# Routing, last rows and send requests of a fused two-layer kernel moved to the ends of attention steps

## The chip, the cores and the metric

The kernel runs on one core of one Trainium2 chip. The metric is the device time of one execution in microseconds; for the kernel before, the median of three runs. Five engines work side by side: TensorE (PE; its weight loads are PEld), VectorE (DVE), ScalarE (ACT), GpSimd (POOL) and SyncE (SP), which issues most of the DMAs.

## What is computed

The reference is two layers on 4096 tokens (8 batches of 512) of width 256. Each layer normalizes its rows and adds an attention-like block and a mixture of experts to them:

```python
xn = _layernorm(x, axis=-1)
x = x + _L0_attn_ref(xn, ...) + _L0_ffn_ref(xn, ...)
xn = _layernorm(x, axis=-1)
x = x + _L1_attn_ref(xn, ...) + _L1_ffn_ref(xn, ...)
return x
```

The first layer's block is a two-directional state-space scan, its experts take one of eight per token. The change concerns the second layer. Its attention has 16 heads of width 16, with keys and values that pass through a latent of width 64:

```python
latent_kv = (k + v) @ W_down_kv
k_rec = latent_kv @ W_up_k
v_rec = latent_kv @ W_up_v
scores = clip(einsum('bhqd,bhkd->bhqk', qh, kh) * scale) * decay
attn = softmax(clip(scores), axis=-1)
out = einsum('bhqk,bhkd->bhqd', attn, vh)
return out @ Wo
```

Its mixture of experts takes the two best of eight per token; the eighth is a "no operation" that returns the token itself, weighted. Each of the seven real experts takes at most 512 tokens, in order of their index:

```python
weights_flat = softmax(x @ router_w.T + router_b, axis=-1)
topk_vals, topk_idx = top_k(weights_flat, 2)
sorted_indices = argsort(-expert_mask, axis=0)[:cap]
h = relu(einsum('ceh,ehi->cei', inputs, experts_inter))
out = einsum('cei,eih->ceh', h, experts_out) * in_w[..., None]
combined = zeros_like(x_flat).at[used_idx].add(out)
combined = combined + x_flat * (noop_w * noop_mask)[:, None]
```

## The kernel before, in words

All data are 32-bit floats. A tile holds 128 tokens (32 tiles, four per batch). The order of instructions on every engine is the order in which Python emits them: generators are advanced by hand, one piece (from one `yield` to the next) at a time, and each engine works its own instructions off in that order, waiting where an operand is not ready.

**The end of the first layer.** `late()` (L512 to 594) finishes the rows of each batch: it adds the gathered expert output (L549), takes mean and variance (L551, L552), writes the rows `x1` (L560), normalizes (square root L159 on ScalarE, L164 to L169 and L567 on VectorE), writes the normalized rows `xn1` (L570), transposes them (L575, L576), and projects to the router's logits (`pp` L582, `proj1` L587). The pieces for batch 7 are left when the second layer begins; they are the generator `rest`.

**The attention steps.** The second layer's loop (L1411 to L1468) goes over 128 steps n = (batch b, head group g of four heads, query tile c), and three more to drain. A step issues, in order: the scores of step n (`scores`, L1277: four matmuls `s_ps` L1284 into four PSUM banks, on VectorE four clips L1289, four products with the decay `band` with a running maximum L1291, and one negation `ng` L1295); one piece of each running `divide` chain; `follow()`; then the exponentials of step n-1 on ScalarE (`exps`, L1299), the transposes of step n-2 (`p_ps` L1306 on TensorE, copies `pT` L1307 on ScalarE), on every second step the products with V (`o_ps` L1315); and between these three or four calls of `fill()`. A clip frees a PSUM bank for the next step's scores.

**What fills.** `fill()` (L1372) advances the first of three lists: a group that may not be split, `urgent`, `idle`. In `urgent` stand first the batch-7 rows (`last_rows`, L1367, put in at L1407), later `inputs_of(b + 1)` from step n = 8 of each 16 (the next batch's latent `lp` L235, Q, K and V; the Q and K rows are stored and read back by `spread`, L1173, one store and 16 small DMAs on SP each), and `finish(b)` (L1224, output projection `fin` L1228, sum L1232). `idle` gets the experts. All these use one PSUM tile with the tag "bank", `bufs=1`: a new use waits until the last reader of the previous one is done.

**Routing and sending.** `follow()` (L1389) does nothing until the batch-7 rows are done. Then each call advances `route1()` (L1074) by one piece: bias and softmax (`softmax_experts`, L174; the exponential L180 on ScalarE), the first maximum (`first_max`, L186), the second, the mask, the ranks (`ranks`, L198: two matmuls `both` L203 and L204 into "bank", a copy of the totals L206, a running sum over tiles L211 and L212, and a last read of `both` in L217), and twice the slots and weights (L1112 to L1116). When routing is done, each call advances `send_rows()` (L1190) twice. Its first piece asks on SP for all eight batches of both `x1` (L1200) and `xn1` (L1197), 512 KB each; each further piece takes a tile: a copy of its slots (`at`, L1221), two indirect DMAs on POOL into `xd1` (L1208), and on VectorE the no-operation share (L1215), which needs both loads. After the last tile `ready` is set and the first expert's weights and rows are asked for (L1129, L1124).

**The divide chain.** After a head group's last product with V, `divide` (L1321) copies the sums out (`os` L1325), stores them (`od` L1326), two steps of the chain later reads them back (`oT` L1336, `sm` L1337), takes the reciprocal (L1342), stores it (`rd` L1343), reads it back spread over the rows (`rb` L1345), and two steps on multiplies (L1348). Its DMAs stand on SP.

**Experts and the end.** From step `ready + 2` the experts are in `idle`: transposes `e_tp` L1144, `e_hp` L1151, `e_yp` L1164. When nothing is left to fill, `more()` (L1385) advances `combine()` (L1242): two gathers on POOL per tile (L1249); the additions (`add`, L1260, at L1263) lag seven tiles behind, and the last seven tiles' 14 additions come in one go.

Of the kernel before, what the change touches and what calls it, by code (L numbers as in the profile page):

```python
# [49 lines left out]
def bc(ap, axis, shape):  # L50

    return ap.unsqueeze(axis).to_broadcast(shape)
# [3 lines left out]
def tile_kernel(ctx: ExitStack, tc: tile.TileContext, t, out: bass.AP):  # L56
# [54 lines left out]
    def rows_of(src, b):  # L111
        return src[b * S : (b + 1) * S, :].rearrange("(c p) d -> p c d", p=P)
# [61 lines left out]
    def softmax_experts(pool, logits, bias):  # L174
        pr = pool.tile(E3, FP, name="pr", tag="pr")
        V.tensor_tensor(pr, logits, bc(bias, 1, E3), ALU.add)
        m = pool.tile([P, NTILE], FP, name="sm_m", tag="sm_m")
        V.tensor_reduce(m, pr, AX.X, ALU.max)
        V.tensor_tensor(pr, pr, bc(m, 2, E3), ALU.subtract)
        A.activation(pr, pr, AF.Exp)  # L180
        V.tensor_reduce(m, pr, AX.X, ALU.add)
        V.reciprocal(m, m)
        V.tensor_tensor(pr, pr, bc(m, 2, E3), ALU.mult)
        return pr

    def first_max(pool, pr, tag):  # L186

# [7 lines left out]
        V.tensor_tensor(oh, bc(i, 2, E3), bc(iota_e, 1, E3), ALU.is_equal)  # L195
        return m, oh

    def ranks(pool, bank, mask):  # L198

        flat = mask.rearrange("p t e -> p (t e)")  # L200
        both = bank("both", [P, 2, NTILE * NE], 1)
        pre, tot = both[:, 0, :], both[:, 1, :]
        T.matmul(pre, row_lt, flat, start=True, stop=True)  # L203
        T.matmul(tot, ones, flat, start=True, stop=True)  # L204
        total = pool.tile(E3, FP, name="rk_t", tag="rk_t")
        V.tensor_copy(total, tot.rearrange("p (t e) -> p t e", e=NE))  # L206
        cum = total
        sh = 1
        while sh < NTILE:
            nxt = pool.tile(E3, FP, name="rk_c", tag="rk_c", bufs=2)  # L210
            V.tensor_copy(nxt[:, 0:sh, :], cum[:, 0:sh, :])  # L211
            V.tensor_tensor(nxt[:, sh:, :], cum[:, sh:, :], cum[:, : NTILE - sh, :], ALU.add)  # L212
            cum = nxt
            sh *= 2
        rank = pool.tile(E3, FP, name="rk_r", tag="rk_r")
        V.tensor_tensor(rank, cum, total, ALU.subtract)
        V.tensor_tensor(rank, rank, pre.rearrange("p (t e) -> p t e", e=NE), ALU.add)  # L217
        n = pool.tile([P, NE], FP, name="rk_n", tag="rk_n")
        V.tensor_copy(n, cum[:, NTILE - 1, :])
        return rank, n  # L220
# [98 lines left out]
    def bank(name, shape, tag="gen"):  # L319
        return mp.tile(shape, FP, name=name, tag=("e", "s")[tag] if isinstance(tag, int) else tag, bufs=2)  # L320
# [4 lines left out]
    def route():  # L325
# [49 lines left out]
        V.tensor_tensor(da, dt, bc(ea, 1, D3), ALU.mult)  # L375


        pr = softmax_experts(big, proj[:, :, 2 * NH :], br)
        m, oh = first_max(big, pr, "a")
        V.tensor_copy(gate, m)  # L380
        rank, n = ranks(big, bank, oh)
        over = big.tile([P, NE, NTILE], FP, name="over", tag="over")
        V.tensor_tensor(over, bc(n, 2, [P, NE, NTILE]), bc(iota_t, 1, [P, NE, NTILE]), ALU.is_gt)
        nb = big.tile([P, NE], FP, name="nb", tag="nb")
# [61 lines left out]
    with ExitStack() as es:  # L446
# [509 lines left out]
        with tc.manual_schedule(engines=ENGINES):  # L956
# [34 lines left out]
            def fill(n):  # L991
                for _ in range(n):
                    if next(rows, "end") == "end":
                        next(rest, None)
# [69 lines left out]
    with tc.tile_pool(name="a1", bufs=1) as p1, tc.tile_pool(name="a2", bufs=2) as p2, tc.tile_pool(  # L1064
# [9 lines left out]
        def route1():  # L1074

            nonlocal r1b, noop
            tls.close()
            big = r1b = r1s.enter_context(tc.tile_pool(name="r1b", bufs=1, side="right"))
            noop = r1b.tile([P, NTILE], FP, name="noop", tag="noop")
            pr = softmax_experts(big, proj1, rb)  # L1080
            yield
            m1, oh1 = first_max(big, pr, "a")

            rest = big.tile(E3, FP, name="rest", tag="rest")
            V.tensor_scalar(rest, oh1, -2.0, None, ALU.mult)
            V.tensor_tensor(rest, rest, pr, ALU.add)
            yield
            m2, oh2 = first_max(big, rest, "b")
            yield
            mask = big.tile(E3, FP, name="mask", tag="mask")  # L1090
            for m, oh in ((m1, oh1), (m2, oh2)):
                pos = big.tile([P, NTILE], FP, name="pos", tag="pos")
                V.tensor_scalar(pos, m, 0.0, None, ALU.is_gt)
                V.tensor_tensor(oh, oh, bc(pos, 2, E3), ALU.mult)
            V.tensor_tensor(mask, oh1, oh2, ALU.add)
            yield
            rank, _ = ranks(big, lambda name, shape, tag: bank(name, shape), mask)
            yield


            V.tensor_tensor(noop, pr[:, :, NE1], mask[:, :, NE1], ALU.mult)


            valid = big.tile(E3, FP, name="valid", tag="valid")
            V.tensor_scalar(valid, rank, float(CAP), None, ALU.is_lt)
            G.memset(valid[:, :, NE1 : NE1 + 1], 0.0)
            base = big.tile([P, NE], FP, name="base", tag="base")
            V.tensor_scalar(base, iota_e, float(CAP), float(NE * CAP - NSLOT1), ALU.mult, ALU.add)
            V.tensor_tensor(rank, rank, bc(base, 1, E3), ALU.add)
            for k, (m, oh) in enumerate(((m1, oh1), (m2, oh2))):  # L1110
                yield
                V.tensor_tensor(oh, oh, valid, ALU.mult)  # L1112
                sl = slots_of(big, oh, rank, "k")
                V.tensor_scalar(sl, sl, float(NSLOT1), None, ALU.add)
                V.tensor_copy(slot1[:, :, k], sl)
                V.tensor_copy(wsel[k], slots_of(big, oh, pr, "w"))  # L1116
# [73 lines left out]
        def send_rows():  # L1190

            sent = []
            rows = {}

            def ask(b):
                rows[b] = r1b.tile([P, TPB, DM], FP, name="xs", tag="xs", bufs=B)
                Y.dma_start(out=rows[b], in_=rows_of(xn1, b))  # L1197

            for b in range(B):
                Y.dma_start(out=x_sb[:, b * TPB : (b + 1) * TPB, :], in_=rows_of(x1, b))  # L1200
                ask(b)
            yield
            for i in range(NTILE):
                b, c = i // TPB, i % TPB
                x = rows[b][:, c, :]
                at = turn(r1b, i)
                for k in range(2):
                    one = G.indirect_dma_start(  # L1208
                        out=xd1, out_offset=bass.IndirectOffsetOnAxis(ap=at[:, k : k + 1], axis=0),
                        in_=x, in_offset=None, bounds_check=NSLOT1 - 1, oob_is_err=False,  # L1210
                    )
                    for other in sent:
                        tc.declare_no_dep(one.ins, other.ins, reason="rows go to slots of their own")
                    sent.append(one)
                V.scalar_tensor_tensor(x_sb[:, i, :], x, noop[:, i : i + 1], x_sb[:, i, :], ALU.mult, ALU.add)  # L1215
                yield
# [139 lines left out]
        with tc.manual_schedule(engines=ENGINES):  # L1356
# [4 lines left out]
            urgent, idle, chains = [], [], []  # L1361
            rows, routing, sends, work, ready, e1 = combine(), route1(), send_rows(), None, None, None

            half_done = []
            late_left = True

            def last_rows():  # L1367
                nonlocal late_left
                yield from rest
                late_left = False  # L1370

            def fill():  # L1372

# [9 lines left out]
                return False  # L1383

            def more():  # L1385
                if ready is not None and n > ready + 2:
                    next(rows, None)

            def follow():  # L1389

                nonlocal work, ready, e1, e2
                if late_left:
                    return
                if next(routing, "end") != "end":
                    return
                for _ in range(2):
                    if next(sends, "end") == "end" and ready is None:
                        ready = n
                        r1s.close()
                        e1 = es.enter_context(tc.tile_pool(name="f1", bufs=1, side="right"))  # L1400
                        e2 = es.enter_context(tc.tile_pool(name="f2", bufs=2, side="right"))
                        work = experts()
                        next(work)

            steps = [(b, g, c) for b in range(B) for g in range(4) for c in range(TPB)]
            N = len(steps)
            urgent.append(last_rows())  # L1407
            done = []
            pT, op, pair = {}, {}, None
            inputs = {0: got}  # L1410
            for n in range(N + 3):  # L1411
# [17 lines left out]
                for chain in list(chains):  # L1429
                    if next(chain, "end") == "end":  # L1430
                        chains.remove(chain)
                follow()
                if ready is not None and n == ready + 2:
                    idle.append(work)
                begun = n >= 1
                if begun:
# [29 lines left out]
                    fill() or more()  # L1466
                if 1 <= n <= N:
                    done[n - 1].exps((3,))  # L1468
            while fill() or chains:
                for chain in list(chains):  # L1470
                    if next(chain, "end") == "end":
                        chains.remove(chain)
# [76 lines left out]
```

## Time and profile before

| | us |
|---|---|
| three runs | 2246.86, 2250.88, 2252.46 (median 2250.88) |
| the profiled execution | 2233.12 |
| its span | 2231.4 |
| PE busy | 1935.2 (87%) |
| DVE busy | 1499.0 (67%) |
| ACT busy | 1070.2 (48%) |
| POOL busy | 689.8 (31%) |
| attention steps begin | 1172.2 |
| `ng` of step 0, 28, 111, 127 | 1182.39, 1432.18, 2088.73, 2198.03 |

The profile is of one execution. Its page gives the busy time of each engine, the span in 40 slices with each engine's busy tenths and the granted TensorE clock, the chain of waits that ended last, and the costliest groups of instructions. Other views give the same for a stretch of time, and the timeline lists instructions with the idle time before them and what ended it. The second layer's attention takes 1172 to 2231 us. `ng` (L1295) is issued once per step and so marks the steps.

### The profile page before, as it was taken

The page shows a single profiled execution, that of the slowest core. Times are in us where ns is not written, and L with a number is a line of the kernel's source. Part 1 is how long each engine was busy: PE and PEld are TensorE (multiplying, and loading weights), DVE is VectorE, ACT ScalarE, POOL GpSimd, SP SyncE. Part 2 cuts the span into 40 slices and gives each one's busy share as a digit, 9 for nine tenths or more (in the row PEclk, how much of TensorE's full clock was granted, in tenths as well). Part 3 has the DMA queues.
Part 4 walks back from the last instruction along what each step waited for, and adds up shares of the span by engine and source line. Part 5 has one row for each costly group of instructions (what it writes and reads, how often), then busy time and mean ns, then how long its engine had stood idle before and what let it go on. Part 6 is the DMA issues. An engine that isn't in the chain of part 4 may idle for free. (4 is left out here: it accounts for less than half of the span.)

```text
span 2231.4 us, 32949 instructions
## 1 busy us (share of the span) xinstructions
PE 1935.2 (87%) x11772; PEld 1281.0 (57%) x11772; DVE 1499.0 (67%) x3323; ACT 1070.2 (48%) x1978; POOL 689.8 (31%) x588
## 2 busy tenths in 40 slices
PE   6559999999998999987867768899999999999885
PEld 5325666667766676644544334565656656565543
DVE  4835766657585665678646679565666767676895
ACT  2223332323233242333324546676667777777764
POOL 0075554546364463655420035200000000000452
PEclk9879999999999999997885878799999999999978
DMA  7134544545454464343432161312213222222255
GB/s 263 38 103 160 174 157 162 193 141 203 139 172 150 132 212 143 128 128 114 157 100 67 37 212 61 96 53 84 71 46 101 82 67 78 58 86 58 90 110 97
DMA packets 156357, 263.61 MB, mean 118 GB/s; under 512 B 25146, under 2 KB 112622, under 8 KB 144290
## 3 DMA queue, kind: packets, MB, share of 16 engines
q1 hardware_dynamic: 124544, 144.65, 20.9%
q0 software_dynamic: 22320, 107.55, 14.9%
q10 hardware_dynamic: 9330, 9.31, 1.2%
q8 instruction: 93, 1.52, 0.3%
q14 instruction: 70, 0.57, 0.1%
HBM read 193.39 MB, written 72.75 MB: 119 GB/s over the span
## 5 line engine op out<-in xcount | busy, mean ns | idle before, releaser
L1289 DVE TENSOR_SCALAR s<-s_ps 128x512 f32<-128x512 f32 x512 | 317.4, 681 | 255.9 <-PE s_ps L1284 209.0
L1299 ACT ACTIVATE s<-s,ng 128x512 f32<-128x512 f32 x512 | 355.3, 727 | 51.7 <-DVE ng L1295 50.1
L1306 PE MATMUL p_ps<-ident,s 128*128 128x128 f32 x2048 | 296.0, 289 | 60.5 <-ACT pT L1307 60.5
L1306 PEld LDWEIGHTS p_ps<-ident,s 128*128 128x128 f32 x2048 | 244.7, 147 | 143.7 <-ACT pT L1307 94.3
L1291 DVE CUSTOM_DVE_ANT_0 s<-s,band 128x512 f32<-128x512 f32 x512 | 322.3, 683 | 0.0
L1307 ACT COPY pT<-p_ps 128x512 f32<-128x512 f32 x512 | 277.8, 591 | 56.3 <-PE p_ps L1306 52.1
L1249 POOL DMA_INDIRECT yg<-yd,at x64 | 67.6, 1056 | 700.6 <-PE s_ps L1284 654.3
L667 PE MATMUL pj<-xT,w_in 128*128 128x512 f32 x384 | 194.6, 632 | 19.4 <-DVE cv L680 18.3
L1284 PE MATMUL s_ps<-kT,qT 16*128 16x512 f32 x1024 | 181.5, 706 | 22.6 <-DVE s L1289 16.5
L486 PEld LDWEIGHTS h_ps<-xdT,w 128*128 128x128 f32 x1248 | 151.6, 195 | 32.6 <-issue 18.0
L486 PE MATMUL h_ps<-xdT,w 128*128 128x128 f32 x1248 | 156.7, 280 | 9.4 <-ACT xdT L476 8.3
L499 PE MATMUL y_ps<-w,hT 128*128 128x256 f32 x624 | 149.3, 382 | 0.7 <-DVE hT L495 0.7
L680 DVE SCALAR_TENSOR_TENSOR cv<-pj,w_conv_w,cv 128x511 f32<-128x511 f32 (+2 forms) x192 | 143.1, 745 | 7.4 <-ACT cv L676 3.4
L1315 PE MATMUL o_ps<-pT,vt 128*32 128x256 f32 x2048 | 143.2, 424 | 0.0
L898 POOL TENSOR_TENSOR yT<-yT,ex 128x512 f32<-128x512 f32 (+1 forms) x48 | 59.4, 1237 | 254.1 <-DVE ex L897 191.6
L499 PEld LDWEIGHTS y_ps<-w,hT 128*128 128x128 f32 x624 | 116.9, 192 | 35.7 <-issue 20.3
L887 DVE TENSOR_TENSOR yT<-yT,yd 128x512 f32<-128x512 f32 (+1 forms) x64 | 43.7, 682 | 122.6 <-PE yd L878 122.5
L667 PEld LDWEIGHTS pj<-xT,w_in 128*128 128x128 f32 x384 | 71.6, 200 | 92.1 <-issue 81.9
L1151 PE MATMUL e_hp<-e_xdT,e_w 128*128 128x256 f32 x448 | 122.4, 396 | 2.3 <-ACT e_xdT L1145 1.9
L835 POOL TENSOR_TENSOR au<-da,row_le 128x1024 f32<-128x1024 f32 x32 | 62.5, 1954 | 195.0 <-DVE end L387 94.1
L1164 PE MATMUL e_yp<-e_w,e_hT 128*128 128x256 f32 x448 | 120.0, 390 | 0.2
L855 ACT ACTIVATE mt<-seg 128x1024 f32<-128x1024 f32 x64 | 65.6, 1024 | 106.7 <-PE seg L850 106.6
(261 smaller groups left out, 3219.0 us busy)
## 6 DMA issues: line engine op xcount, KB each, us to landing
ex<-exd SPq DMA_DIRECT2D x96, 128.0 KB
u<-in_u_dram SPq DMA_DIRECT2D x16, 512.0 KB
xtd<-xT SPq DMA_DIRECT2D x16, 512.0 KB
fr<-fdd SPq DMA_DIRECT2D x64, 128.0 KB
od<-os SPq DMA_DIRECT2D x32, 256.0 KB
xT<-xtd SPq DMA_DIRECT2D x15, 512.0 KB
e_w<-in_ei_dram SPq DMA_DIRECT2D x7, 1024.0 KB
e_w<-in_eo_dram SPq DMA_DIRECT2D x7, 1024.0 KB
```

The lines of the kernel that those rows point to most:

```text
L486: T.matmul(hp[:, i, :], w1[:, k * FF + f * P : k * FF + (f + 1) * P], xdT[:, k * P : (k + 1) * P], start=(k == 0), stop=(k == KC - 1),)
L499: T.matmul(yp, hT[f // 4][:, f % 4, :], w2[:, f * DM : (f + 1) * DM], start=(f == 0), stop=(f == FC - 1))
L667: T.matmul(pj, w_in[:, k, o * P : (o + 1) * P], self.xT[:, k, :], start=(k == 0), stop=(k == KC - 1))
L680: V.scalar_tensor_tensor(cv[:, s:], pj[:, : S - s], conv_w[:, q, 3 - s : 4 - s], cv[:, s:], ALU.mult, ALU.add)
L1151: T.matmul(hp, w1[:, k, f * P : (f + 1) * P], xdT[:, k, :], start=(k == 0), stop=(k == KC - 1))
L1284: T.matmul(sp[i], self.q[r, cols], self.k[r, :], start=True, stop=True)
L1289: V.tensor_scalar(self.p[i], sp[i], -CLAMP, CLAMP, ALU.max, ALU.min)
L1291: V.tensor_tensor_reduce(out=self.p[i], in0=self.p[i], in1=band[:, at : at + S], scale=1.0, scalar=-3.0e38, op0=ALU.mult, op1=ALU.max, acc ...
L1299: A.activation(self.p[i], self.p[i], AF.Exp, bias=self.ng[:, i : i + 1])
L1306: T.transpose(pp[:, k, :], self.p[i][:, k * P : (k + 1) * P], ident)
L1307: A.copy(pT[i][:, :, cc * P : (cc + 1) * P], pp)
L1315: T.matmul(op[32 * i : 32 * i + 32, half * 2 * P : (half + 1) * 2 * P], self.v[:, k, h * (AD + 1) : h * (AD + 1) + 32], pT[i][:, k, :], st ...
```

## The change

Four things are moved or altered; the arithmetic stays the same.

1. `follow()` is called at the end of a step, after the last exponential, instead of before the fills. While batch-7 rows are left, it advances them itself, two pieces per step (`LATE`), so that they no longer stand in `urgent`; their first piece (the request for rows) is emitted before step 0.
2. `softmax_experts` yields ahead of its exponential. `route1` is cut anew, into six pieces instead of eight: the first maximum goes with the rest of the softmax; the second maximum with the mask; the ranks with the first part of the slots.
3. `ranks` copies all of `both` to SBUF at once (`hold` gives the place) and works from the copy.
4. `send_rows` asks for two batches at first, and for batch b + 2 when it comes to batch b's first tile. `xn1` is asked for ahead of `x1`.

The experts start at `ready + 3`, and `more` from `ready + 4`, since `ready` is now set at the end of a step.

```diff
@@ softmax_experts
         V.tensor_tensor(pr, pr, bc(m, 2, E3), ALU.subtract)
+        yield
         A.activation(pr, pr, AF.Exp)
...
-        return pr
+        yield pr
@@ ranks
-    def ranks(pool, bank, mask):
+    def ranks(pool, bank, mask, hold):
...
-        pre, tot = both[:, 0, :], both[:, 1, :]
-        T.matmul(pre, row_lt, flat, start=True, stop=True)
-        T.matmul(tot, ones, flat, start=True, stop=True)
-        total = pool.tile(E3, FP, name="rk_t", tag="rk_t")
-        V.tensor_copy(total, tot.rearrange("p (t e) -> p t e", e=NE))
+        T.matmul(both[:, 0, :], row_lt, flat, start=True, stop=True)
+        T.matmul(both[:, 1, :], ones, flat, start=True, stop=True)
+        held = hold([P, 2, NTILE * NE])
+        V.tensor_copy(held, both)
+        pre, total = (held[:, k, :].rearrange("p (t e) -> p t e", e=NE) for k in range(2))
@@ route1
-            pr = softmax_experts(big, proj1, rb)
+            chances = softmax_experts(big, proj1, rb)
+            next(chances)
             yield
+            pr = next(chances)
             m1, oh1 = first_max(big, pr, "a")
+            yield
...
             V.tensor_tensor(rest, rest, pr, ALU.add)
-            yield
             m2, oh2 = first_max(big, rest, "b")
-            yield
...
-            rank, _ = ranks(big, lambda name, shape, tag: bank(name, shape), mask)
-            yield
+            rank, _ = ranks(
+                big, lambda name, shape, tag: bank(name, shape), mask,
+                lambda shape: big.tile(shape, FP, name="rk_b", tag="rk_b"),
+            )
@@ send_rows
             def ask(b):
                 rows[b] = r1b.tile([P, TPB, DM], FP, name="xs", tag="xs", bufs=B)
                 Y.dma_start(out=rows[b], in_=rows_of(xn1, b))
-
-            for b in range(B):
                 Y.dma_start(out=x_sb[:, b * TPB : (b + 1) * TPB, :], in_=rows_of(x1, b))
+
+            for b in range(2):
                 ask(b)
             yield
             for i in range(NTILE):
                 b, c = i // TPB, i % TPB
+                if c == 0 and b + 2 < B:
+                    ask(b + 2)
@@ the loop of attention steps
+            LATE = (2, 2, 2, 2, 2)
...
-            def last_rows():
+            def last_rows(k):
+
                 nonlocal late_left
-                yield from rest
-                late_left = False
+                for _ in range(k):
+                    if next(rest, "end") == "end":
+                        late_left = False
...
             def more():
-                if ready is not None and n > ready + 2:
+                if ready is not None and n > ready + 3:
                     next(rows, None)
...
                 if late_left:
+                    last_rows(LATE[n])
                     return
...
-            urgent.append(last_rows())
+            last_rows(1)
...
-                follow()
-                if ready is not None and n == ready + 2:
+                if ready is not None and n == ready + 3:
                     idle.append(work)
...
                 if 1 <= n <= N:
                     done[n - 1].exps((3,))
+                follow()
```

The first layer's use of `softmax_experts` and `ranks` is adapted to the new signatures; there the whole copy goes into one of the existing row buffers.

More of the change, by code (lines that the diff above doesn't have):

```diff
@@ L216, in ranks @@
         V.tensor_tensor(rank, cum, total, ALU.subtract)
-        V.tensor_tensor(rank, rank, pre.rearrange("p (t e) -> p t e", e=NE), ALU.add)
+        V.tensor_tensor(rank, rank, pre, ALU.add)
         n = pool.tile([P, NE], FP, name="rk_n", tag="rk_n")
@@ L375, in route @@
         V.tensor_tensor(da, dt, bc(ea, 1, D3), ALU.mult)
-        pr = softmax_experts(big, proj[:, :, 2 * NH :], br)
+        _, pr = softmax_experts(big, proj[:, :, 2 * NH :], br)
         m, oh = first_max(big, pr, "a")
         V.tensor_copy(gate, m)
-        rank, n = ranks(big, bank, oh)
+        rank, n = ranks(big, bank, oh, lambda shape: row("rk_b").rearrange("p (a b) -> p a b", a=2))
         over = big.tile([P, NE, NTILE], FP, name="over", tag="over")
```

## The prediction

> **What bounds the kernel now.** I read the page's slices first, then the stages' table, then the chain of waits over 1140 to 1440 us, and last the timeline around each long piece of it.
>
> ```profile
> span 2231.4 us, 32949 instructions
> ...
> PE   6559999999998999987867768899999999999885
> ...
> PEclk9879999999999999997885878799999999999978
> ```
>
> Slices 22 to 26, some 1172 to 1437 us, are the weak spot: TensorE is 6 to 8 tenths busy at a granted clock of 5 to 8 tenths. That is the start of the second layer, attention steps 0 to 28, before its experts have begun: the stage that the change rearranges. The stages' table says what bounds what follows (after the range: length, then busy us of PE, PEld, DVE, ACT, POOL, then clock, DMA share, GB/s):
>
> ```profile
> 1244.00:1333.00 89.00, 58.49 (x357) 31.49 (x360) 55.94 (x164) 41.42 (x76) 14.59 (x15) 0.77 0.47 148
> ...
> 1437.00:2089.00 652.00, 626.12 (x4476) 409.62 (x4480) 435.50 (x1115) 470.35 (x905) 4.26 (x4) 0.98 0.22 71
> 2089.00:2232.00 143.00, 103.84 (x745) 59.87 (x736) 116.20 (x315) 84.69 (x153) 63.30 (x60) 0.84 0.53 107
> ```
>
> From 1244 to 1333 nobody is full: waits. From 1437 to 2089, with experts, TensorE is full (626 of 652), so moving work there saves nothing. After 2089 VectorE leads. The chain of waits names the waits of the first stage:
>
> ```profile
> 1248.34 6.75 issue
> 1255.09 3.54 PE lp L235 x4
> ...
> 1291.53 6.81 DMA xs<-xn
> ...
> 1313.32 8.43 DMA rd<-sm
> 1321.77 4.38 DMA rb<-rd
> ```
>
> The timeline shows who stands there (brackets: idle time just before, and what ended it):
>
> ```profile
> 1218.34 0.42 ACT L180 ACTIVATE pr<-pr 128x256 f32<-128x256 f32 x1 [7.45 <-issue]
> ...
> 1254.57 0.42 DVE L217 TENSOR_TENSOR rk_r<-rk_r,both 128x256 f32<-128x256 f32 x1
> 1255.09 3.54 PE L235 MATMUL lp<-xT,w_kv 128*64 128x512 f32 x4 [6.76 <-issue]
> ...
> 1298.44 0.48 DVE L1215 SCALAR_TENSOR_TENSOR x_sb<-xs,noop,x_sb 128x256 f32<-128x256 f32 x1 [6.02 <-DMA xs<-xn]
> ...
> 1326.27 0.69 DVE L1348 TENSOR_TENSOR oT<-oT,rb 128x512 f32<-128x512 f32 x1 [10.13 <-DMA rb<-rd]
> ...
> 1437.08 1.09 PE L1144 MATMUL e_tp<-ident,e_xd 128*128 128x128 f32 x4 [5.67 <-DMA rd<-sm]
> ...
> 2198.11 5.06 DVE L1263 SCALAR_TENSOR_TENSOR x_sb<-yg,wsel,x_sb 128x256 f32<-128x256 f32 x11
> ```
>
> ScalarE stands 7.45 us at the routing's exponential; TensorE 6.76 us because the one PSUM tile "bank" is held until VectorE has read `both` a last time (L217); VectorE 6.02 us for the first rows to send, then 10.13 us for `rb`, queued behind 16 loads of 512 KB; TensorE 5.67 us for the first expert's rows. The last line matters later: a burst of leftover additions, now after the last step's scores (its `ng` is at 2198.03), where nobody waits for it.
>
> [...] So an ask behind a waiting issue on SP waits too; SP's long waits here (60.7 us in two waits for `qc`) fit. [...] eight `s_ps` took 3.86 us after 6.87 us idle, 1.14 us when warm.
>
> **The change, part by part.** I use each step's `ng` (L1295, end of a step's scores on VectorE): before, ng0 1182.39, ng1 1187.42, ng5 1229.18, ng7 1244.36, ng8 1251.07, ng9 1273.13, ng12 1303.80, ng15 1332.78, ng27 1426.67, ng28 1432.18, ng111 2088.73, ng127 2198.03. "lp" is the start of the matmuls at L235, before 1255.09. A step's scores are 4 x 0.62 clip, 4 x 0.61 product and 0.17, 5.0 us on VectorE.
>
> *Late rows.* They now stand behind step 0's scores instead of step 1's. Their load `xr` is issued by SP at 1181.67 and landed at about 1185.5 (SP's own wait for it), so VectorE waits 3.0 us that it did not wait before; then 4.5 us of sums and 5.0 of scores: ng1 1195.1 (+7.7). The square root stands after the exponentials; its input comes at 1190 as VectorE's scores begin, so it is done before they are. Then 2.4 us of normalizing: ng2 1202.5. The two transposes now stand back to back ahead of step 3's `s_ps`, the second waiting for ScalarE to empty the one bank: these end at some 1203, ng3 1208.5. In step 3 TensorE does 16 `p_ps` (4 us, cold) and `pp` (3.4) first: ng4 1218.1 (+1.4). Ends: 4 us less if TensorE is warm (its 16 `p_ps` then take 2.2), 2 more if `xr` lands only at 1187.5, when VectorE used it without a wait.
>
> *Softmax split.* Its exponential runs after step 4's last one (inputs ready), so the 7.45 us go and what is late next is TensorE's transposes: with `o_ps` (3.1) and `p_ps` (4) step 5's clips begin at 1222.2, ng5 1227.2 (-2.0). Then 3.3 us (normalize, first maximum) and 4.6 us (second, mask) on top of the scores: ng6 1235.9, ng7 1245.6 (+1.2).
>
> *Ranks.* The two matmuls move to the end of step 7. VectorE copies all of `both` right after ng7 (0.6 us, of which the total alone was 0.42 before), and the bank is free at 1246.4: lp 1246.4, 8.7 us earlier. The copy's extra 0.2 us is hidden by step 8's matmuls.
>
> *Asks.* Here a wait is added. Routing ends in step 9 instead of 11, so tile 0 is taken in step 9. But the asks stand on SP behind the K rows' store and 16 spreading DMAs of steps 8 and 9. Before, these were all issued at lp+32.4; for the next batch (lp 1387.68) at lp+31.4. I take lp+32. First landing: before, 1290.75 to 1298.44, 7.7 us; VectorE goes on at about lp+39.5. Without the asks it would reach step 10's scores at lp+25 (the next batch: 1412.72). So it stands some 18 us, 15 of them on the path; queued behind are step 10's clips, then TensorE's step 11 scores, whose banks they free. Ends: 11 us less if loads land before SP's issues suggest; 5 more if all six loads (3.1 MB at 286 GB/s, 10.5 us, plus 2) land together. With 0.5 for the tile and 5.0 of scores, ng10 is lp+45 = 1291.5; two steps of 6 us later ng12 1303.4, against 1303.80. So the time won before lp is spent. The 3.0 us of `xr` and this wait are the change's two new waits.
>
> *`rb`.* Now two loads, not 16, stand ahead of its chain: the 10.13 us go (what is late next is VectorE itself: steps of 6.0, scores and two tiles). [...] ng15 1322.5, 10.3 us earlier. Steps 16 to 27 are unchanged (sends end two steps earlier, but steps 24 to 27 are bound by TensorE). ng27: about 1416.5.
>
> *Experts.* The last sends are in step 25 instead of 27, experts start in step 28 instead of 29. Their rows are asked for at lp+32 of batch 2, land 5.5 us later; e_tp's turn is lp+38: its 5.67 us go. Step 28's 5.5 us without experts goes too, but the experts end a step earlier, so one more step falls to the last stage. Which? The built programs' order shows that the 14 leftover additions then stand *before* step 127's scores. At 0.48 us, 6.7, with gather waits 7.8 (before: 2198.11 to 2205.9): ng127 is 12.9 us after ng126, where a bare step is 5.2. Sum: -5.5 - 5.7 + 12.9 = +1.7. Low end: the gathers landed earlier, +0.6; high: wait 3 us more, +4.7.
>
> POOL's 64 sends (1.28 us apart, two tiles 5.1 us per step) keep their step; the ACT queue loses no DMA and gains none.
>
> **The sum.** -10.3 + 1.7 = -8.6 us. The profiled execution took 2233.12 us (2231.4 span, 1.7 around it), so 2224.5; it lies 0.8% under the median of the three runs, 2250.88. I put the same 8.6 us on the median: 2242.
>
> **Rivals.** Differences under about 0.3% (6.8 us) can't be told from none here.
>
> Forecast, gain 3 to 16 us (2235 to 2248), 0.48.
>
> More: the loads land early enough that tile 0 hardly stalls. For: asks need nothing of K, and the trace has SP's issues only by batch 2's pattern. Against: SP issues in order. Up to 14 us more: 2228. 0.20.
>
> No change: tile 0 waits for all six loads (5 us) and the burst at the end costs 3 us more: 2250. 0.16.
>
> Slower: one mechanism, tile 0's loads. If they move at the stage's mean 148 GB/s instead of 286, 3.1 MB need 21 us and VectorE goes on at lp+55, 15.5 us after my value: 2258. For: they run beside the K spreads' small packets; against: the same loads reached 286 to 365 GB/s in 1290 to 1316. It decides from lp+48; slower by 0.3% from lp+55. 0.16. (That the change doesn't do what it says is excluded by the order of its instructions.)
>
> **Numbers.** Faster by over 0.3% means a gain above 6.8: 0.34 of the forecast's share and the 0.20, 0.54; within: 0.14 and 0.15, 0.29; slower 0.17. The range runs from the second case's 2228 to 2257, just inside the slow rival's time; some 0.10 is left out above and 0.08 below.
>
> **What would show it.** Right: no idle above 1 us before the routing's exponential; lp near 1246; a VectorE wait of 15 to 20 us at `x_sb<-xs` in step 9; none above 2 us at `oT<-oT,rb` of batch 0; no wait at e_tp; 14 additions ahead of the last scores. Wrong: lp later than 1252, tile 0's wait under 8 or over 25 us, or a last stage that is not longer by a step.

## The result and the profile after

The changed kernel took 2237.65 us (median of 14 runs, 2222.94 to 2242.67) beside 2251.33 of the kernel before (14 runs): a ratio of 0.993, 95% interval [0.9906, 0.9953]. It is faster by 0.7%; the forecast was 2242, a ratio of 0.996. Repeated later on two chips, called B and C below, it gave 0.9973 [0.9953, 0.9993] and 0.9977 [0.996, 0.9995]; on which chip the first comparison was made is not on record.

The profiled executions alone would mislead: 2233.12 us before and 2234.56 after. Before's is lower than any of its 14 timed runs, so the two may not come from the same chip. So I compare stages, and in the experiments executions on one chip. First the slices of the page after:

```profile
span 2232.8 us, 32938 instructions
...
PE   6659999999999999987867877999999999999785
...
PEclk9879999999999999997886678899999999999886
```

The weak stretch, slices 22 to 26, is still there: its clock digits are 6, 6, 7, 8, 8, where before has 5, 8, 7, 8, 7. At the other end the last slices show TensorE at a lower granted clock (8, 8, 6 for 9, 7, 8). The timeline names the pieces (in brackets idle time just before, and what ended it):

```profile
1181.12 0.48 DVE L550 SCALAR_TENSOR_TENSOR xr<-yg,gate,xr 128x256 f32<-128x256 f32 x1 [3.25 <-DMA xr<-x]
...
1217.06 0.45 ACT L181 ACTIVATE pr<-pr 128x256 f32<-128x256 f32 x1
...
1236.45 3.67 PE L236 MATMUL lp<-xT,w_kv 128*64 128x512 f32 x4 [1.17 <-DVE rk_b L206]
...
1274.07 0.48 DVE L1221 SCALAR_TENSOR_TENSOR x_sb<-xs,noop,x_sb 128x256 f32<-128x256 f32 x1 [16.43 <-DMA x_sb<-x]
...
1307.53 0.69 DVE L1354 TENSOR_TENSOR oT<-oT,rb 128x512 f32<-128x512 f32 x1
...
1415.38 1.09 PE L1148 MATMUL e_tp<-ident,e_xd 128*128 128x128 f32 x4 [2.53 <-DMA e_xd<-xd]
...
2185.32 6.50 DVE L1269 SCALAR_TENSOR_TENSOR x_sb<-yg,wsel,x_sb 128x256 f32<-128x256 f32 x14
```

Line by line against before: VectorE now waits for the late rows' load; ScalarE no longer stands at the routing's exponential; TensorE waits 1.17 us for the bank instead of 6.76; VectorE stands 16.43 us for the first rows to send instead of 6.02; `oT` follows the scores with no wait, where it was 10.13; `e_tp` still waits 2.53; and 14 additions now lie ahead of step 127's scores. Why the rows are late is read from SP's queue (start of issuing and its length, line, transfer, count):

```profile
1250.19 7.27 SPq L1183 DMA_DIRECT2D qT<-qd  x16
1257.56 0.38 SPq L253 DMA_DIRECT2D kd<-kc  x1
1260.93 7.32 SPq L1183 DMA_DIRECT2D kT<-kd  x16
1268.56 0.38 SPq L1201 DMA_DIRECT2D xs<-xn  x1
```

3.0 us pass between the issue of the K rows' store `kd<-kc` and the first spread, which reads `kd`; 2.9 of them are SP's wait for that store, and in them SP issues nothing of what stands behind. The 16 spreads then take 7.3 us to issue. The first ask goes out as soon as the sixteenth is issued, at lp + 32.1. VectorE had wanted the rows since 1257.6.

**Milestones** make the gain countable, in us after the second layer's first spread (`qT<-qd`). The last two columns are from one chip, A: the kernel before again, and an experiment (spread additions) that has the changed kernel's order up to the leftover additions at the end.

| | before | after | before, chip A | spread additions, chip A |
|---|---|---|---|---|
| lp | 82.9 | 68.7 | 79.3 | 68.9 |
| ng9 | 100.9 | 86.9 | 97.4 | 87.1 |
| ng12 | 131.6 | 123.6 | 127.4 | 124.3 |
| ng15 | 160.6 | 149.4 | 156.0 | 143.1 |
| ng27 | 254.5 | 245.7 | 249.0 | 231.6 |
| first `e_tp` | 264.9 | 247.6 | 259.7 | 233.4 |
| last `e_yp` ends | 908.0 | 891.1 | 900.6 | 874.0 |
| end | 1059.2 | 1065.0 | 1053.7 | 1034.0 |

The 10 to 14 us won by lp shrink to 3 to 8 at ng12, behind tile 0's wait. The `rb` wait's end adds to them at ng15: 9.8 us on A, but only 3.2 in the first pair, where VectorE now waits for TensorE instead. Steps 13 to 15 of the changed kernel, first in the first pair, then in the spread additions on A (length, busy us of PE, PEld, DVE, ACT, POOL with their counts, granted clock, DMA share, GB/s):

```profile
1291.40:1317.20 25.80, 22.95 (x128) 13.31 (x132) 18.84 (x53) 18.16 (x31) 11.94 (x12) 0.60 0.61 202
```

```profile
1290.40:1309.20 18.80, 14.42 (x120) 7.95 (x116) 18.70 (x55) 14.79 (x27) 12.38 (x12) 0.94 0.81 263
```

VectorE does the same 18.8 us of work; at a clock of 0.60 it waits 6.9 us for the scores, at 0.94 not at all. The experts take the same time in all columns (640 to 644 us), so what is won ahead of them is kept; what is spent after them is the last stage: 151.2 us before, 173.9 after, and on chip A 153.1 and, without the burst, 160.0.

### The profile page after: what moved, and what is told of

The parts are those of the page before. It is cut to its first block, busy times and chain, and to the rows that moved or that the text cites. A ratio compares the mean times of both kernels' runs of the same rounds, so it can differ in the third digit from the quotient of the medians.

```text
span 2232.8 us, 32938 instructions
## 1 busy us (share of the span) xinstructions
PE 1950.2 (87%) x11772; PEld 1286.6 (58%) x11772; DVE 1497.2 (67%) x3323; ACT 1074.0 (48%) x1978; POOL 689.4 (31%) x588
## 5 line engine op out<-in xcount | busy, mean ns | idle before, releaser
L1312 PE MATMUL p_ps<-ident,s 128*128 128x128 f32 x2048 | 305.6, 295 | 65.4 <-ACT pT L1313 48.3
L1312 PEld LDWEIGHTS p_ps<-ident,s 128*128 128x128 f32 x2048 | 251.4, 150 | 155.2 <-ACT pT L1313 77.6
L1321 PE MATMUL o_ps<-pT,vt 128*32 128x256 f32 x2048 | 148.8, 433 | 1.8 <-issue 1.8
```

Of the source, the lines that this page charges most:

```text
L1312: T.transpose(pp[:, k, :], self.p[i][:, k * P : (k + 1) * P], ident)
L1321: T.matmul(op[32 * i : 32 * i + 32, half * 2 * P : (half + 1) * 2 * P], self.v[:, k, h * (AD + 1) : h * (AD + 1) + 32], pT[i][:, k, :], st ...
```

## The experiments

My theory after the result: the change wins some 10 us up to lp, hands most of it to tile 0's wait, wins the `rb` wait and the experts' earlier start, and pays part back in the last stage. The rivals: one piece alone made the gain (the asks two batches ahead, or the freed bank); the new waits cost nothing; or the order in the attention stage, and not these waits, decides. The experiments ran on three chips, each beside runs of the kernel before: A (before 2229.0 us), B (2248.45), C (2252.81). The changed kernel itself ran on B and C, not on A. The ratios expected ahead of the runs on A and B take 0.993 for the changed kernel; on B and C it was 0.997 to 0.998.

**The kernel before again (A).** Without an edit.

> The kernel before, unchanged, profiled once more. The first profile of it took 2233.12 us, less than any of its 14 timed runs (2238.82 to 2267.12). Theory A (that execution was a lucky one, and the usual one loses time in the attention steps that the change rearranges): the new profile takes 2245 to 2255 us, and the extra 12 to 20 us show before the first expert step, where TensorE runs cold. Theory B (the extra is spread over the whole span through the granted clock): no stage stands out, each is some 0.5 to 0.8% longer.

2230.17 us, with ng at the third column's times. Its waits: `rb` 9.8 us, first rows 5.4, lp 6.76, `e_tp` 5.9, all within 0.7 of the prediction's. The first pair's before was 4.6 us later at ng15 than this one, with the same order: single profiles differ that much. Neither theory came true: this execution was not longer than the first profile, and the 24 timed runs of before on this chip have a median of 2229.0 us.

**All loads asked for at once, as before (A).**

```diff
                 Y.dma_start(out=rows[b], in_=rows_of(xn1, b))
-                Y.dma_start(out=x_sb[:, b * TPB : (b + 1) * TPB, :], in_=rows_of(x1, b))
...
-            for b in range(2):
+            for b in range(B):
+                Y.dma_start(out=x_sb[:, b * TPB : (b + 1) * TPB, :], in_=rows_of(x1, b))
                 ask(b)
...
-                if c == 0 and b + 2 < B:
-                    ask(b + 2)
```

> The changed kernel with the asks as before: all eight batches at once, the residual rows ahead of the normalized ones. Theory [...]: VectorE stands about 10 us at the product with rb of batch 0 once more, the first tile's wait stays 16 to 18 us, so 7 to 10 us slower than the changed kernel (ratio to before 0.996 to 0.998). Rival (the asks don't matter, since the wait for rb falls together with other waits): within 2 us of the changed kernel, ratio 0.993.

2224.81 us, ratio 0.9981 [0.997, 0.9991]. The queue of 16 loads again holds up the divide chain, in another of its transfers than before:

```profile
1309.15 0.35 DVE L1346 RECIPROCAL sm<-sm 128x32 f32<-128x32 f32 x1 [12.11 <-DMA sm<-od]
1321.35 0.69 DVE L1352 TENSOR_TENSOR oT<-oT,rb 128x512 f32<-128x512 f32 x1
```

VectorE stands 12.11 us at `sm`, one transfer earlier in the chain, and none at `rb`; ng12 to ng15 takes 31.0 us, where the spread additions' run took 18.8. Tile 0's wait is 16.14 us with the other loads and 17.03 without (spread additions). So the asks two batches ahead are worth about 12 us of wait in this order, and do nothing for tile 0. In the whole that is some 13 us, more than the 7 to 10 expected (an estimate: 2224.81 less 2207.02 of the spread additions, less the 4.6 us of their burst).

**Only the asks two batches ahead, the rest as before (B).**

```diff
-            for b in range(B):
+            for b in range(2):
                 ask(b)
...
+                if c == 0 and b + 2 < B:
+                    ask(b + 2)
```

(with `x_sb`'s load moved into `ask`.)

> The kernel before, with the asks alone changed: two batches at first, then two ahead. Theory (the wait for rb behind 16 loads is the largest single gain of the change, 10 us): ratio 0.995 to 0.997, no idle time at the product with rb, the first tile's wait 5 to 7 us as before. Rival (tiles now wait for rows asked for too late): x_sb waits show in later steps and the ratio is 0.998 or more.

2244.0 us, ratio 0.9979 [0.9961, 0.9997].

```profile
1296.99 0.48 DVE L1217 SCALAR_TENSOR_TENSOR x_sb<-xs,noop,x_sb 128x256 f32<-128x256 f32 x1 [6.05 <-DMA x_sb<-x]
...
1314.62 0.69 DVE L1350 TENSOR_TENSOR oT<-oT,rb 128x512 f32<-128x512 f32 x1
```

The `rb` wait is gone, and no later tile waits for its rows, as the rival had it; the first rows' 6.05 us stay, since the routing ends where it ended. This part alone gives 4.5 us by the medians, just short of the expected 0.995 to 0.997 and less than the 10.13 us of the wait removed. Part of the rest is seen: in ng12 to ng15 VectorE waits 3.3 us for TensorE's scores instead, at a granted clock of 0.64, and the stretch takes 22.2 us for 29.0 and 28.6 in the two profiles of before. Where the remainder went isn't shown, since before was not profiled on this chip.

**The ranks' bank held to the end again (B).** `ranks` reads its two products from PSUM as before, everything else is the changed kernel.

```diff
-        V.tensor_copy(held, both)
...
+        V.tensor_copy(total, tot.rearrange("p (t e) -> p t e", e=NE))
...
-        V.tensor_tensor(rank, rank, pre, ALU.add)
+        V.tensor_tensor(rank, rank, pre.rearrange("p (t e) -> p t e", e=NE), ALU.add)
```

> The changed kernel, with ranks reading the PSUM tile to its end as before (only the totals are copied first). Theory: the bank comes free some 3 to 4 us later, the next batch's first matmuls start that much later, and since the asks on SP and so tile 0's wait follow them, all of it shows: 3 to 4 us slower than the changed kernel (ratio 0.994 to 0.995). Rival (the copy changes nothing, since the rest of TensorE's work of step 8 hides it): same as the changed kernel within 1 us.

```profile
1238.42 3.65 PE L236 MATMUL lp<-xT,w_kv 128*64 128x512 f32 x4 [4.39 <-issue]
```

2242.64 us, ratio 0.9981 [0.9959, 1.0002]; the changed kernel on the same chip 2240.55, 0.9973. lp's wait is 4.39 us instead of 1.17, and ng9 to ng12 are 3.3 to 3.4 us later than in the changed kernel: the copy is worth 3 us where it acts. In the whole the two intervals overlap: the expected 3 to 4 us are neither shown nor excluded, 2 us can't be told apart.

**The changed kernel again (B).**

> The changed kernel itself, to be measured beside its variants on the same chip. Ratio to before 0.993 (0.990 to 0.995).

2240.55 us, ratio 0.9973, above the expected 0.990 to 0.995. ng9 87.1, a wait of 16.4 us for tile 0, ng12 123.6: as in the first profile to 0.2 us. `e_tp` waits 1.1.

**The first two batches asked for early (A).** The one new wait of 16 us comes from the place of the asks in SP's queue. Two lines move them ahead of the K and Q spreads, to the end of step 6:

```diff
             def follow():
...
+                if n == 6:
+                    next(sends)
```

> The changed kernel with the asks for batches 0 and 1 issued at the end of step 6, ahead of the next batch's Q and K spreads, instead of behind them in step 9. Theory (tile 0's wait of 16.4 us comes from SP's order, and 14 us of it are on the path): the wait goes and the kernel is 10 to 14 us faster than the changed one, ratio to before 0.987 to 0.989. Rival (the time is lost anyway, since TensorE is the bound in steps 8 to 11): at most 4 us faster, ratio 0.991 to 0.993.

2197.64 us, ratio 0.9855 [0.983, 0.9881], a little more gain than expected.

```profile
1259.64 0.48 DVE L1221 SCALAR_TENSOR_TENSOR x_sb<-xs,noop,x_sb 128x256 f32<-128x256 f32 x1
...
1263.63 2.48 DVE L1295 TENSOR_SCALAR s<-s_ps 128x512 f32<-128x512 f32 x4 [3.03 <-PE s_ps L1290]
```

Tile 0 is taken with no wait at all. What is late next is TensorE, 3.03 us at step 10's scores and 2.91 at step 11's, so of the 16 us some 13 are won at ng10 (98.7 for 112.4 and 111.4 in this chip's two kernels with the stall) and 10.6 at ng12 and ng15 (113.7 and 132.5 against the spread additions' 124.3 and 143.1). The wait was on the path, and its cause was SP's order, not the memory; the rival, that TensorE would lose the time anyway, fell.

**The leftover additions one at a time (A, and again on C beside the changed kernel).**

```diff
             for one in held:
+                yield
                 add(*one)
```

> The changed kernel with the last seven tiles' additions in pieces of one tile, so that four and not fourteen of them stand ahead of the last step's scores. Theory: 10 additions of 0.48 us leave the path, 4 to 5 us faster than the changed kernel, ratio to before 0.990 to 0.992. Rival (the tail waits for something else, so nothing is won): ratio 0.993.

```profile
2159.37 1.91 DVE L1270 SCALAR_TENSOR_TENSOR x_sb<-yg,wsel,x_sb 128x256 f32<-128x256 f32 x4
...
2166.24 4.66 DVE L1270 SCALAR_TENSOR_TENSOR x_sb<-yg,wsel,x_sb 128x256 f32<-128x256 f32 x10
```

2207.02 us, ratio 0.99 [0.9878, 0.9921]. Four additions now lie ahead of step 127's scores and ten behind them, where nobody waits: ng127 follows ng126 by 7.5 us, where the two kernels of this chip with the burst took 12.1. But the total is 22 us below before, much more than 4.6, and ng12 to ng27 was 107.3 us here where the changed kernel had taken 122 to 124. Was it this edit, which touches no instruction ahead of the last additions, or the chip? The pair on C answers.

> The changed kernel again, as the common base of the three others on one chip. Theory (the time won ahead of the asks is handed back at tile 0's wait): ratio to the kernel before 0.993 to 0.998; ng9 87, a wait of 16 to 17 us, ng10 112, ng12 123.5 after the second layer's start, ng127 12 us after ng126. Steps 13 to 27 are where the runs so far differ for one and the same order of instructions (107 us from ng12 to ng27 in two runs, 122 to 124 in two): if the chip decides that, this run's number is shared by the others of this call; if the order decides, it is 122 to 124 here and 107 in the spread additions' run.

> The changed kernel with the last stage's leftover additions one at a time. Theory: the last two steps' ng are 7 to 8 us apart instead of 12, so it is 4 to 7 us faster than the changed kernel of the same call (ratio to the kernel before lower by 0.002 to 0.003), and ng0 to ng27 are the same as in the changed kernel within 2 us wherever TensorE's granted clock is the same. Rival, the order of the additions also shortens steps 13 to 27: ng12 to ng27 then is 107 us here against 122 in the changed kernel, and the gain 20 us.

On C the changed kernel took 2244.3 us, 0.9977 [0.996, 0.9995], and the spread additions 2240.87, 0.9944 [0.9922, 0.9967]: 3.4 us less, just under the expected 4 to 7, with ng126 to ng127 10.2 us for 13.2 (7 to 8 and 12 were expected). The intervals still touch. And ng12 to ng27 is 126.8 and 128.9 us, nearly the same for both: the rival falls. The same order took 107 us on A. Stretches ng12 to ng27 (columns as above), first the spread additions on A:

```profile
1290.40:1397.70 107.30, 89.22 (x632) 47.75 (x624) 91.55 (x259) 75.75 (x139) 54.72 (x54) 0.89 0.36 114
```

The same kernel on C:

```profile
1300.90:1429.80 128.90, 105.47 (x640) 58.28 (x640) 92.18 (x257) 80.93 (x143) 54.18 (x54) 0.75 0.32 98
```

VectorE does the same 92 us of work. TensorE's granted clock is 0.89 in one and 0.75 in the other, its same matmuls take 89 and 105 us, and VectorE's waits for TensorE's scores grow from 13.9 to 27.1 us. On A, a step's eight `s_ps`:

```profile
1325.22 1.14 PE L1291 MATMUL s_ps<-kT,qT 16*128 16x512 f32 x8
```

and on C some way on in the same stage:

```profile
1352.95 2.09 PE L1291 MATMUL s_ps<-kT,qT 16*128 16x512 f32 x8
```

**Both edits (B).** Early asks and spread additions together.

> The changed kernel with both mends: the asks for batches 0 and 1 at the end of step 6, and the last additions in pieces of one tile. Theory: the two are in different places and add up: early asks alone gave 0.9855, the pieces alone 0.990, so against 0.993 for the changed kernel 0.982 to 0.983. Rival (the second hides what the first wins): 0.985 or more.

2223.52 us, ratio 0.9886 [0.9851, 0.9921], 17.0 us below the changed kernel of the same chip. No stall at tile 0; ng12 112.3 for 123.6. It is faster than both kernels of this study, by 1.1% than before. The expected 0.982 to 0.983 was missed, and the ratio lies where the rival put it (0.985 or more). That does not show that one edit hides the other: the expected figure adds up ratios from A, and the 17.0 us on this chip are about the sum of the two gains (some 14 on A by estimate, 3.4 on C). Neither edit ran alone on B.

**The softmax's exponential in one piece with its inputs (C).**

```diff
         V.tensor_tensor(pr, pr, bc(m, 2, E3), ALU.subtract)
-        yield
         A.activation(pr, pr, AF.Exp)
+        yield
```

> The changed kernel, with the softmax's exponential issued in one piece with its inputs, ahead of the step's last attention exponential on ScalarE. Theory (the split is worth what it removes): ScalarE stands 6 to 8 us at the routing's exponential again, ng5 and all up to ng12 are 4 to 6 us later, lp too; the whole is 3 to 6 us slower than the changed kernel of the same call. Rival, tile 0's wait decides when the rows go: the lateness is absorbed there, ng10 unchanged and the whole the same within 2 us.

```profile
1220.22 0.42 ACT L180 ACTIVATE pr<-pr 128x256 f32<-128x256 f32 x1
```

My theory for this part fell. No wait returned; ng0 to ng12 are those of the changed kernel on B to 0.2 us, and within 2 us of it on C; 2244.84 us, 0.9951 [0.9928, 0.9975], beside 2244.3 of the changed kernel: not slower. The rival, that the lateness is absorbed at tile 0, fell too: there was no lateness. What removes the 7.45 us then is, as I read it, `follow()` at the end of the step: its pieces stand behind the step's last exponential, not ahead of it as my theory said. VectorE's subtraction is done at some 1219.5, 0.7 us before ScalarE comes to the routing's exponential, so the split has nothing to hide. `follow()` was not put back alone, so this is argued from the order and from the other parts, not shown by a run of its own.

**The late rows in their old places (C).** `last_rows` a generator in `urgent` again, the routing still begun after step 4:

```diff
-                if late_left:
-                    last_rows(LATE[n])
+                if late_left or n < 4:
                     return
...
-            last_rows(1)
+            urgent.append(last_rows())
```

> The changed kernel, with the last eight rows' sums and normalizing worked off in the old places (between the products of steps 0 to 3) and the routing begun after step 4 as in the changed kernel. Theory (moving these rows is worth nothing itself, it only makes room for the routing to be begun): no wait at xr, ng1 15 instead of 22.7, ng3 35 as in both kernels, ng5 50 to 53, ng9 to ng12 within 2 us of the changed kernel, the whole within 3 us. Rival, the move itself is what made steps 4 and 5 short: ng5 56 to 57, everything up to ng12 7 us later, the whole 5 to 7 us slower.

2242.58 us, ratio 0.9942 [0.992, 0.9964]. No wait at `xr`; ng1 14.9, ng5 47.1, ng9 84.0, ng12 121.2: 1 to 3 us ahead of the changed kernel on this chip (ng5 48.0, ng9 86.1, ng12 124.4), and earlier than the 50 to 53 that I had expected at ng5. So moving the late rows wins nothing up to ng12 and costs at most 3 us; the rival, that it made steps 4 and 5 short, fell. By ng27 the lead is gone (254.4 for 251.2, at a granted clock of 0.76 for 0.78 from ng12 on), and in the whole it can't be told from the changed kernel (1.7 us by the medians).

## Why the prediction was right, step by step

**The kind and the size.** Forecast −8.6 us; measured −13.7 in the first comparison, −7.9 on B and −8.5 on C. The mechanism was right in the main. Of the signs that were named ahead, these came: no wait at the routing's exponential, 16.43 us at `x_sb<-xs` in step 9, none at `oT<-oT,rb`, and 14 additions ahead of the last scores. lp came earlier than named, and `e_tp` still waited 2.53 us. That the sum came so close is in part luck: several terms were off by 4 to 10 us each, in both directions, and the first pair's traces add up to +5.8 us, those of A to an estimated −15, with −8.6 between them. The terms, against the milestones:

- *Late rows*: 3.0 us of wait at `xr`, measured 3.25; ng1 +7.7, measured +7.5.
- *Steps 2 to 5*: mis-sized. I put ng5 2.0 us earlier and ng7 1.2 later; they came 7.3 and 4.4 earlier. The term that was mis-sized is "TensorE does 16 `p_ps` (4 us, cold) and `pp` (3.4)": ng4 came at 41.9 for my 45.9. Step 5's `o_ps` and `p_ps` are priced cold too, and ng5 came at 49.7 for 55.0. Before, in this stretch (`p_ps` x8, then `pp`):

```profile
1202.72 1.91 PE L1306 MATMUL p_ps<-ident,s 128*128 128x128 f32 x8
1204.42 3.42 PE L582 MATMUL pp<-w_w_r,xT 128*128 128x8 f32 x16
```

After, the same matmuls:

```profile
1197.95 1.09 PE L1312 MATMUL p_ps<-ident,s 128*128 128x128 f32 x8
...
1200.86 1.85 PE L583 MATMUL pp<-w_w_r,xT 128*128 128x8 f32 x16
```

They ran warm: the granted clock was 1.00 under this `pp`, where it was 0.50 under before's. I had named that as the low end, "4 us less if TensorE is warm", and taken the cold value. So lp came 14.2 us earlier for my 8.7 in the first pair. On A it came 10.4 earlier: there before was in part warm too (`pp` 1.85 us), and after had `p_ps` cold (3.76 for 16) and `pp` warm (1.89). The 3.86 us that I gave for eight `s_ps` after idle time are not the clock's doing alone: they ran at a granted clock of 0.50 (before, from 1299.58 on), but their four pairs start 0.6 us apart, as VectorE's clips of 0.62 us free their banks one by one. Started together, eight took 2.09 us at 0.50 (1307.76) and 1.14 at 1.00 (1275.61).

- *Softmax split*: the wait went, as said, but not by the split; `follow()`'s place is what is left to have done it.
- *Ranks*: held. The bank costs 3.3 us when it is not freed.
- *Tile 0's wait*: asks at lp + 32 (measured 32.1), VectorE on at lp + 39.5 (37.6), a stall of "some 18 us" (16.4). Tile 0 did not wait for all six loads either: it went on 5.5 us after the first ask, and 3.1 MB at 350 GB/s take 9 us (an estimate; so were the 2 us that I added for landing: SP waited up to 2.4 us in before and 2.9 in after for a store, `qd<-qc` or `kd<-kc`, to land). The slow rival, loads at 148 GB/s, fell; in 40 slices of 1265 to 1290 us they moved some 350 and more:

```profile
GB/s 53 98 59 62 82 66 53 72 88 377 382 387 352 356 346 346 351 346 349 354 359 349 405 371 262 98 232 54 154 62 164 213 326 347 361 357 397 225 210 38
```

The rival with more gain, loads that land early, was not what happened; the early asks made it happen, and it then was worth about what it was put at: some 14 us on A (an estimate: 2207.02 of the spread additions and 4.6 of their burst, less 2197.64), and on B 17.0 with the spread additions' share, some 3, in it.

- *`rb`*: −10.3 at ng15, measured −11.2 in the first pair and −12.9 on A. In the first pair that agreement is luck: ng12 was at −8.0 for my −0.4, and the three steps after it gave 3.2 us for my 9.9. "What is late next is VectorE itself" failed there: it is TensorE, at a clock of 0.60, for which VectorE waits 6.9 us. On A the term held: −3.1 at ng12, and 9.8 us in the three steps.
- *"Steps 16 to 27 are unchanged"*: failed in both directions. From ng15 to ng27 before took 93.9 us and, on A, 93.0; after took 96.3, and on A the same order 88.5. On B and C, with the stall at tile 0, it was 101 to 109. On A it is a gain of 4.5 us that I had put at nothing because TensorE bounds steps 24 to 27. Most of it lies in ng23 to ng27 (39.2 us for 43.1), where the sends now end two steps earlier; but before with only the asks changed took 40.1 there on B, so that cause is not shown.
- *Experts' start*: −21.4 by my sum; −17.3 in the first pair, −26.3 on A. `e_tp`'s 5.67 us did not go for sure: in runs of the same order it was 1.1 to 2.5 us, and 5.64 in the kernel with the exponential in one piece.
- *Last stage*: +12.9 forecast, 5.2 for the step and 7.7 for the burst. On A +6.9 without the burst, and the burst 4.6: +11.5. The burst is smaller since before's own last step took 7.6 us and not 5.2. In the first pair +22.7: 10.2 up to ng111 for the one step more, 5.3 over ng111 to ng126, 4.5 for the burst, 2.7 after ng127. TensorE's granted clock is 0.82 from ng111 to ng127, where before has 0.86; on A, where the stage is 6.9 us longer, little more than the step is left.

**What stays open.** In the first pair the second layer is 5.8 us *longer* after than before (1065.0 for 1059.2), though the runs say 13.7 us shorter. Like pairs on A give −19.7 with the spread additions, so about −15 with the burst (an estimate: −19.7 + 4.6). The profiled execution of before behaves like chip A's, that of after like B's and C's; that is read from ng12 to ng27 and not shown, since before was not profiled on B and C. Its 2233.12 us lie within A's timed runs of before (2220.29 to 2235.79) and below all of C's. Nor is it shown why the same order keeps a clock of 0.89 on A and 0.75 on C. The change seems to pay some clock itself: over its timed runs the mean granted clock is 0.9128 where before has 0.9184 (B), and 0.9115 for 0.9151 (C); with the stall at tile 0 gone (both edits, B) it is 0.9177. On C, 0.01 of clock goes with some 16 us of time (one slope through the timed runs, each kernel's taken from its own mean), so 0.0036 would be some 6 us of the gain. That is an association; which of the two follows from the other is not shown. The changed kernel with its late rows in their old places has 0.9154 on C, the clock of before: moving them may be what costs it.

## What to carry to other kernels

When a piece of work is moved forward, ask what its transfers stand behind on the issuing queue: here the rows were asked for behind a wait of 3.0 us for a store and 16 small DMAs that took 7.3 us to issue, and of the 10 to 14 us won ahead of it 6 to 7 were lost to a stall that two lines remove. An edit of two parts can be right for a reason other than the one it is named after, so undo each part alone. A sum can come close while its terms miss, so check the forecast stage by stage. And where a stage is held by one engine while TensorE is only partly busy, price its matmuls at both clocks that the trace shows (eight `p_ps`: 1.09 and 1.91 us here), and compare totals only on one chip.

## What the runs showed of the hardware

- The same kernel before took 2229.0 us (24 runs) on A, 2248.45 (59 runs) on B and 2252.81 (61 runs) on C: 1.1% between the lowest and the highest, more than the change is worth. Each chip was used at one time only, so chip and time can't be told apart here. On A the runs were also closer together, 2220.29 to 2235.79, than on C, 2240.88 to 2268.64. Where the difference lies is seen for one order only: the spread additions' spans on A and C differ by 33.4 us, 21.6 of them in ng12 to ng27, 11.8 in the last stage and 11.2 in the first layer, while the experts went 9.1 faster on C. The first layer took 1166 to 1177 us in all profiles.
- Idle time of TensorE alone does not tell its granted clock in these traces. At the first pair's tile-0 stall, after 5.85 us idle, the clock was 0.50 from 1275.2 to 1285.5, and eight `s_ps` took 2.09 us there. But it was 0.50 ahead of the stall too, from 1254 to 1266, where TensorE was busy all 12.0 us. From ng12 to ng27 the spread additions on C kept a mean clock of 0.75, with one idle time of 2.88 us before its first matmuls and none above 2.08 us after that; on A it was 0.89, with idle times up to 2.26 us. TensorE was busy 82% and 83% of it. What sets the stage on C apart from A's is open.
- The asks' lateness was not the memory's here: six loads of 512 KB arrived while the DMA engines moved some 350 GB/s, the first in use 5.5 us after its issue, but their issue had waited in line for 11 us after VectorE stood.
